# Perceiver, two layers on one core: normed rows, softmax sums, key spreading and sine transfers of layer 0 in another order

## The chip, the cores and the metric

The kernel runs on 1 core of one Trainium2 chip. The metric is the device time of one execution in microseconds (us). The core has five engines that run side by side, each with its own queue of instructions, worked off strictly in order: TensorE (PE in the profile), VectorE (DVE), ScalarE (ACT), GpSimd (POOL) and SyncE (SP, which here only starts transfers). They wait for each other through semaphores.

## The reference, cut to what matters

The model is a perceiver with two layers over x (64 sequences of 32 rows, 256 wide) and a context (64 x 257 rows). Layer 0, which is all that the change touches, is

```python
x = x + xattn(layernorm(x), ctx)      # 16 heads of 16, rotary q and k, a window of 64 keys back
x = x + attn(layernorm(x))            # 16 heads, rotary, causal
x = x + fp8_linear(layernorm(x))
```

With 32 rows in a sequence, both attentions reach only keys 0 to 31 and are causal. Layer 1 (attention over all 257 context rows, a gated mixer, a mixture of 8 experts and a shared one) follows in the same program.

## The kernel before, in words

The 2048 rows of x lie in SBUF as four groups of 512 rows (`xs[0..3]`), each four tiles of 128 rows. `small_attentions` (line 246) does both attentions of layer 0 as one list of eight steps, `order`: four groups of the first attention, then four of the second. A step has four turns, t = 0 to 3; a turn is one 128-row tile.

The program writes the order of every engine out by hand. The loop at line 542 is a software pipeline: a turn computes the scores of tile T, and does the later stages of the tiles before it, held in `line`. Per tile:

- `scores` (392): 8 masks and 32 small matmuls into one pair of PSUM banks ("b34", a single buffer, so the next tile's scores wait until this one's have been read), then on VectorE `mx` (row maximum) and `sc` (subtract it), then on ScalarE `e` (exponential).
- `sums` (434), one turn later: VectorE adds up `e` per head and takes the reciprocal, `sm`.
- `turned` and `context` (440, 452), two turns later: TensorE transposes `e` into `ps_t`, ScalarE copies it (`eT`), 32 matmuls with the values give `ps_o`, VectorE scales it by `sm` into `o`.
- `by_feature` (475), three turns later: `o` is transposed (`ps_c`), ScalarE copies it with a bias (`cT`).
- `project` (487), four turns later: `ps_p`, which VectorE adds to x. `ps_o`, `ps_c` and `ps_p` share two PSUM banks.

Beside this, a step prepares the next one, called `after`. `opened` (298) transposes its normed rows y (`psT`) and ScalarE copies them (`yT`), at t = 0. `rotated` (304) is called four times, (1,0), (1,1) for keys and (0,0), (0,1) for queries: a projection `ps_qk`, then VectorE multiplies it by the sine (`part`), four transfers of 64 KB each move `part` by 32 partitions into `far`, ScalarE copies `ps_qk` to `near`, GpSimd multiplies `near` by the cosine, and one turn later GpSimd adds `near` and `far` into `kT` or `qT`. `spread_keys` (343) writes four masked copies of a piece of `kT` into `kb`, three on ScalarE and one on GpSimd, in two parts per turn. `values` and `blocks` (360, 380) project the values, write them to DRAM (`v_rows`) and load them back in another shape (`vb`).

In the second attention keys come from `yT`; in the first they come from the context, so only its queries need `yT`.

The layer norm is `norm_steps` (123), spread over the four turns of the step two ahead: statistics at t = 0; aggregation and a Newton iteration for the reciprocal root at t = 1 (on GpSimd, except in the first groups, where VectorE does it); normed rows y of tiles 0 and 1 at t = 2, of tiles 2 and 3 at t = 3. With `by_act` ScalarE writes y as x * r + off, where GpSimd has made `off` = -mean * r with two small operations; without it, VectorE writes y = (x - mean) * r. Five of the eight steps (n = 1 to 5) have `by_act`; their rows are opened at the start of steps 2 to 6. Also on VectorE, a few `scratch` operations per step decode the fp8 weights in n = 1 to 4.

Before the loop comes a start (from line 492): loads, normed rows of group 0, its four `rotated` (where VectorE makes `near`, too), the first spreading, both `values`. In these four calls half of the sine transfers are started from ScalarE's queue. `eye`, a small selection matrix that the scores need, is made by VectorE from the constants `cst`, ahead of the first norm.

The turn's order at line 560 is `turned`, `sums`, the first part of `spread_keys`, at t = 0 the owed additions and `opened`, `project`, `rotated`, `by_feature`, the norm's piece, the additions, the second part of `spread_keys`, `values` or `blocks`, `scores`, `context`.

Of the kernel before, what the change touches and what calls it, by code (L numbers as in the profile page):

```python
# [12 lines left out]
ALU = mybir.AluOpType  # L13
# [5 lines left out]
NB, S, SK = 64, 32, 257  # L19
# [45 lines left out]
def perceiver_kernel(ctx: ExitStack, tc: tile.TileContext, a: dict, out: bass.AP):  # L65
# [15 lines left out]
    ident = cst[:, C_ID : C_ID + P]  # L81
# [16 lines left out]
    class InOrder:  # L98
# [12 lines left out]
    vector, scalar, gpsimd, sync = (  # L111
        InOrder(e) for e in (nc.vector, nc.scalar, nc.gpsimd, nc.sync)
    )
# [115 lines left out]
    def proj(ps, w, rhs):  # L229

        for k in range(2):
            mm(ps, lhsT=w(k), rhs=rhs(k), start=(k == 0), stop=(k == 1))
# [13 lines left out]
    def small_attentions(layers, first_loads, decode, sides, load_layer1, layer1):  # L246
# [24 lines left out]
        def mask(which):  # L271
            at = C_CAUSAL[which]
            mk = sb.tile([P, 8, S], BF16, tag=f"lx{which}", name=f"mk{which}")
            scalar.copy(mk, cst[:, at : at + S][:, None, :].to_broadcast([P, 8, S]))
            masks.append(mk)
# [17 lines left out]
        def group(n, kvT):  # L293

            layer, g = order[n]
            return dict(layer, n=n, g=g, kvT=kvT)

        def opened(it):
            yT = transposed(it["y"], pa, yTs([P, 2, GT], "yT"))
            it["yT"] = yT  # L300
            if not it["from_ctx"]:
                it["kvT"] = yT

        def rotated(it, i, c):

            src, cs, sn = (
                (it["kvT"], cos, sin) if i == 1 else (it["yT"], cosq, sinq)
            )
            place = "kT" if i == 1 else "qT"
            if c == 0:  # L310
                it[place] = kT_all if i == 1 else qT_([P, 2, GT], "qT")
            dst = it[place]
            w, v0 = it["w"], it["v0"]
            ps = pa([P, GT], "ps_qk")
            proj(ps, lambda k: w[:, i, k, c * P : (c + 1) * P], lambda k: src[:, k, :])

            def by_place(table):
                return table.rearrange("p (o q) -> p o q", o=1).to_broadcast([P, 16, S])

            def by_seq(tile_):  # L320
                return tile_.rearrange("p (b q) -> p b q", q=S)

            bias = vec[:, v0 + 2 * i + c : v0 + 2 * i + c + 1]
            part = part_([P, GT], "part")
            vector.scalar_tensor_tensor(
                by_seq(part), by_seq(ps), bias, by_place(sn), ALU.add, ALU.mult
            )

            far = far_([P, GT], "far")
            for at in range(0, P, S):  # L330
                queue = scalar if it["n"] == 0 and at >= 2 * S else sync
                queue.dma_start(out=far[at : at + S, :], in_=part[at ^ S : (at ^ S) + S, :])
            near = near_([P, GT], "near")
            if it["n"] > 0:
                scalar.activation(near, ps, AF.Identity, bias=bias)
                gpsimd.tensor_tensor(by_seq(near), by_seq(near), by_place(cs), ALU.mult)
            else:
                vector.scalar_tensor_tensor(
                    by_seq(near), by_seq(ps), bias, by_place(cs), ALU.add, ALU.mult
                )  # L340
            return lambda: gpsimd.tensor_tensor(dst[:, c, :], near, far, ALU.add)

        def spread_keys(it, half, c, part):

            if (c, part) == (0, 0):
                it["kb"][half] = sb.tile(
                    [P, 2, NBT // 2, 4, S], F32, tag=f"kb{half}", name="kb"
                )
            kb, kT = it["kb"][half], it["kT"]
            src = kT[:, c, half * D : (half + 1) * D].rearrange("p (b k) -> p b k", k=S)  # L350
            for h in range(2 * part, 2 * part + 2):
                mine = m4r[:, h : h + 1]
                if h != 1:
                    scalar.activation(kb[:, c, :, h, :], src, AF.Copy, scale=mine)
                else:
                    gpsimd.tensor_scalar(
                        kb[:, c, :, h, :], src, mine, 1.0, ALU.mult, ALU.mult
                    )
# [75 lines left out]
        def sums(tile_s):  # L434
            sm = small.tile([P, H], F32, tag="sm", name="sm", bufs=4)
            vector.tensor_reduce(sm, tile_s["e"], AX.X, ALU.add)
            vector.reciprocal(sm, sm)
            tile_s["sm"] = sm
# [55 lines left out]
        order = [(layer, g) for layer in layers for g in range(NG)]  # L494
# [5 lines left out]
        eye = sb.tile([P, S], BF16, tag="eye", name="eye")  # L500
        loads = first_loads()
        next(loads)
        it = group(0, fetch(0))
# [3 lines left out]
        for half in range(2):  # L507
            clear(vbs[1][half])
        scalar.copy(ident_bf, ident)
        vector.tensor_tensor(eye, ident[:, 0:S], ident[:, 64 : 64 + S], ALU.add)  # L510
        mask(0)
        it["y"] = finish(norm_steps(order[0][1], vector))
        it["kb"] = [None, None]
        adds = [rotated(it, 1, 0)]
        opened(it)
        mask(1)
        steps = norm_steps(order[1][1], vector, apart=True)
        next(steps)
        adds.append(rotated(it, 1, 1))
# [19 lines left out]
        line = [None] * 5  # L539
        adds = []  # L540
        layer1_loads = load_layer1()
        for n in range(len(order) + 1):
            if n >= last:
                after = None
            elif n > 0:
                after = group(n + 1, kvT)
                after["y"] = y
            if after is not None:
                after["kb"] = [None, None]
            kvT = None  # L550
            if n + 2 <= last:
                side = norm_steps(
                    order[n + 2][1], None if n else vector, apart=True, by_act=n > 0
                )
            else:
                side = sides
            y = None
            for t in range(NT):
                if line[2]:
                    turned(line[2])  # L560
                if line[1]:
                    sums(line[1])
                kb_now = None
                if n <= last:
                    if t < 2:
                        kb_now = (now, 1, t)
                    elif after is not None:
                        kb_now = (after, 0, t - 2)
                if kb_now:
                    spread_keys(*kb_now, 0)  # L570
                due, adds = adds, []
                if t == 0:
                    for add in due:
                        add()
                    due = []
                    if after is not None:
                        opened(after)
                if line[4]:
                    project(line[4])
                if after is None:  # L580
                    next(layer1, None)
                elif t > 0:
                    adds.append(rotated(after, *((1, 1), (0, 0), (0, 1))[t - 1]))
                if line[3]:
                    by_feature(line[3])
                if n + 2 <= last:
                    try:
                        next(side)
                    except StopIteration as end:
                        y = end.value  # L590
                else:
                    next(side, None)
                    next(side, None)
                if n > 0:
                    add_bias(n - 1, t)
                if n > 0 and t != 1:
                    next(decode, None)
                for add in due:
                    add()
                if kb_now:  # L600
                    spread_keys(*kb_now, 1)
                if after is None:
                    next(layer1, None)
                elif t == 0:
                    adds.append(rotated(after, 1, 0))
                elif t < 3:
                    values(after, t - 1)
                else:
                    for half in range(2):
                        blocks(after, half)  # L610
                line[0] = scores(now, t) if n <= last else None
                if (n, t) == (last, NT - 1):
                    pair_pool.close()
                    later_psum.append(
                        attention.enter_context(tc.tile_pool(name="at_late", bufs=1, space=PSUM))
                    )
                if line[2]:
                    context(line[2])
                if t == 0 and n + 2 <= last:
                    kvT = fetch(n + 2)  # L620
                elif n < 2:
                    next(loads, None)
                elif n >= last - 2:
                    next(layer1_loads, None)
                line = [None] + line[:-1]
            now = after
# [1415 lines left out]
```

## Time and profile before

| what | value |
|---|---|
| three runs | 946.12, 948.07, 949.11 us (median 948.07) |
| the profiled execution | 949.13 us, its span 947.4 us |
| busy in the span | PE 861.0, DVE 588.5, POOL 501.4, ACT 433.7 us |

| stretch, us | what | PE busy | DVE busy | ACT busy | POOL busy |
|---|---|---|---|---|---|
| 0 to 36 | start, up to the first scores | 20.82 | 18.86 | 9.20 | 13.63 |
| 36 to 62 | step 0 and a stall at its end | 18.43 | 17.60 | 14.09 | 11.81 |
| 62 to 110 | steps 1 and 2 | 45.22 | 33.10 | 28.70 | 30.22 |
| 110 to 215 | steps 3 to 6 | 94.03 | 79.33 | 69.46 | 71.45 |
| 215 to 260 | step 7 and the passage to layer 1 | 38.79 | 34.11 | 19.66 | 20.80 |
| 260 to 781 | rest of layer 0 and layer 1's attention | 494.83 | 364.95 | 261.37 | 284.29 |
| 781 to 947 | experts | 148.88 | 40.58 | 31.27 | 69.23 |

A row of a list of groups or of a timeline gives a start, a duration, the engine, the operation and the tiles that it writes and reads; in brackets stands how long the engine was idle before it and whose work ended that. SPq and ACTq are the engines' transfer-issuing instructions. Matmul ends are modelled, so a busy PE may hide small stalls.

### The profile page before, as it was taken

The page shows a single profiled execution, that of the slowest core. Times are in us where ns is not written, and L with a number is a line of the kernel's source. Part 1 is how long each engine was busy: PE and PEld are TensorE (multiplying, and loading weights), DVE is VectorE, ACT ScalarE, POOL GpSimd, SP SyncE. Part 2 cuts the span into 40 slices and gives each one's busy share as a digit, 9 for nine tenths or more (in the row PEclk, how much of TensorE's full clock was granted, in tenths as well). Part 3 has the DMA queues.
Part 4 walks back from the last instruction along what each step waited for, and adds up shares of the span by engine and source line. Part 5 has one row for each costly group of instructions (what it writes and reads, how often), then busy time and mean ns, then how long its engine had stood idle before and what let it go on. Part 6 is the DMA issues. An engine that isn't in the chain of part 4 may idle for free. (4 is left out here: it accounts for less than half of the span.)

```text
span 947.4 us, 22812 instructions
## 1 busy us (share of the span) xinstructions
PE 861.0 (91%) x8699; PEld 589.2 (62%) x8699; DVE 588.5 (62%) x1733; ACT 433.7 (46%) x1119; POOL 501.4 (53%) x994
## 2 busy tenths in 40 slices
PE   5779889987989999999999999999889889999993
PEld 2546566665546666566666656565566648888882
DVE  4757777788667748766776757678763781121116
ACT  1457666665365545554554546554444222222210
POOL 3447666675395647647565647655651204455430
PEclk9989999999999999999999999999799989999997
DMA  5564332344301111101111113000001035777658
GB/s 156 149 157 130 85 77 75 95 125 147 100 7 51 52 52 51 48 5 52 52 52 51 53 51 95 3 1 2 24 24 35 23 127 170 236 230 243 213 184 266
DMA packets 66718, 88.79 MB, mean 94 GB/s; under 512 B 32400, under 2 KB 49840, under 8 KB 64560
## 3 DMA queue, kind: packets, MB, share of 16 engines
q1 hardware_dynamic: 62768, 77.36, 27.1%
q0 software_dynamic: 3456, 9.44, 3.0%
q8 instruction: 69, 1.13, 0.5%
q10 hardware_dynamic: 384, 0.52, 0.2%
q14 instruction: 41, 0.34, 0.1%
HBM read 65.80 MB, written 13.11 MB: 83 GB/s over the span
## 5 line engine op out<-in xcount | busy, mean ns | idle before, releaser
L106 ACT ACTIVATE e<-e,xnm 128x257 f32<-128x257 f32 x256 | 127.2, 498 | 51.1 <-DVE xnm L106 47.7
L106 DVE CUSTOM_DVE_ANT_0 e<-ps_s,mask 128x257 f32<-128x257 f32 x256 | 93.4, 420 | 50.1 <-PE ps_s L118 49.8
L118 PE MATMUL ps_k<-ct,w_w_l1x 128*128 128x512 f32 x256 | 122.3, 600 | 1.5 <-ACT yT L106 0.5
L118 PE MATMUL ps_v<-w_w_l1x,ct 128*128 128x256 f32 x512 | 121.9, 381 | 0.0
L106 POOL TENSOR_SCALAR e<-e,xsm 128x256 f32<-128x256 f32 x256 | 121.2, 492 | 0.0
L121 PE MATMUL ps_t<-cst,e 128*128 128x128 f32 x640 | 103.2, 284 | 7.8 <-DVE eT L106 6.9
L106 DVE COPY eT<-ps_t 128x512 f32<-128x512 f32 x128 | 87.9, 687 | 28.5 <-PE ps_t L121 28.1
L118 PEld LDWEIGHTS ps_v<-w_w_l1x,ct 128*128 128x128 f32 x512 | 94.0, 192 | 11.0 <-issue 0.2
L106 POOL TENSOR_TENSOR x<-x,rows 128x256 f32<-128x256 f32 x96 | 70.4, 749 | 44.0 <-ACT y L106 16.9
L106 ACT ACTIVATE kT<-ps_k,vec 128x512 f32<-128x512 f32 x64 | 44.0, 688 | 100.8 <-PE ps_k L118 100.5
L121 PEld LDWEIGHTS ps_t<-cst,e 128*128 128x128 f32 x640 | 72.2, 142 | 26.3 <-DVE eT L106 7.6
L106 ACT ACTIVATE hTr<-ps_h,w 128x256 f32<-128x256 f32 (+1 forms) x80 | 31.3, 449 | 115.3 <-issue 88.1
L106 DVE TENSOR_TENSOR og<-ps_o,b 128x512 f32<-128x512 f32 (+1 forms) x20 | 12.8, 638 | 104.5 <-PE ps_o L118 104.5
L118 PEld LDWEIGHTS ps_k<-ct,w_w_l1x 128*128 128x128 f32 x256 | 44.5, 190 | 41.3 <-issue 35.3
L1807 POOL DMA_INDIRECT r_rows<-og,lv x36 | 35.5, 986 | 61.2 <-DVE og L106 56.3
L118 PE MATMUL ps_h<-ygT,w 128*128 128x256 f32 (+1 forms) x320 | 65.8, 359 | 0.6 <-issue 0.6
L118 PE MATMUL ps_o<-w,hTr 128*128 128x256 f32 x288 | 65.3, 379 | 0.0
L106 ACT COPY v<-ps_v 128x512 f32<-128x512 f32 x80 | 46.3, 580 | 39.4 <-PE ps_v L118 37.9
L106 POOL TENSOR_TENSOR near<-near,cst 128x512 f32<-128x512 f32 x28 | 35.9, 1282 | 53.2 <-ACT near L106 51.9
L106 POOL TENSOR_TENSOR last<-e,xsm 128x4 f32<-128x4 f32 x64 | 12.9, 202 | 89.2 <-DVE xsm L106 89.2
L106 ACT ACTIVATE kb<-kT,cst 128x256 f32<-128x256 f32 x96 | 45.3, 513 | 30.9 <-POOL kT L106 20.6
L118 PEld LDWEIGHTS ps_h<-ygT,w 128*128 128x128 f32 x320 | 54.9, 190 | 6.6 <-issue 0.8
(209 smaller groups left out, 1693.2 us busy)
## 6 DMA issues: line engine op xcount, KB each, us to landing
ct<-in_ctxT SPq DMA_DIRECT2D x16, 1024.0 KB
w<-in_ew SPq DMA_DIRECT2D x20, 514.0 KB
w<-in_ew SPq DMA_DIRECT2D x20, 512.0 KB
far<-part SPq DMA_DIRECT2D x120, 64.0 KB
v_rows<-v SPq DMA_DIRECT2D x16, 256.0 KB
vb<-v_rows SPq DMA_DIRECT2D x64, 64.0 KB
r<-r_rows SPq DMA_DIRECT2D x8, 512.0 KB
b<-in_eb SPq DMA_DIRECT2D x20, 128.0 KB
```

The costliest lines, as they stand in the source:

```text
L106: ins = getattr(self.engine, name)(*args, **kw)
L118: return kept(nc.tensor.matmul(ps, **args))
L121: return kept(nc.tensor.transpose(ps, src, eye))
L1807: wrote = nc.gpsimd.indirect_dma_start(out=r_rows, out_offset=bass.IndirectOffsetOnAxis(ap=write_i[:, at : at + 1], axis=0), in_=o[:, i, : ...
```

## The change

Five edits, all in `small_attentions`: all sine transfers of the start go to SP's queue; `eye` is made after the first normed rows, `rotated(1,0)` and `opened`; `by_act` is gone there, so VectorE writes y in every step (GpSimd still does the Newton iteration); in each turn, `sums` comes last, behind `context`, instead of near the top; and at t = 0 the first part of `spread_keys` comes behind the owed additions and `opened`. For t > 0 nothing stands between the old and the new place of `spread_keys`.

```diff
             for at in range(0, P, S):
-                queue = scalar if it["n"] == 0 and at >= 2 * S else sync
-                queue.dma_start(out=far[at : at + S, :], in_=part[at ^ S : (at ^ S) + S, :])
+                sync.dma_start(out=far[at : at + S, :], in_=part[at ^ S : (at ^ S) + S, :])
...
         scalar.copy(ident_bf, ident)
-        vector.tensor_tensor(eye, ident[:, 0:S], ident[:, 64 : 64 + S], ALU.add)
         mask(0)
         it["y"] = finish(norm_steps(order[0][1], vector))
         it["kb"] = [None, None]
         adds = [rotated(it, 1, 0)]
         opened(it)
         mask(1)
+        vector.tensor_tensor(eye, ident[:, 0:S], ident[:, 64 : 64 + S], ALU.add)
...
-                side = norm_steps(
-                    order[n + 2][1], None if n else vector, apart=True, by_act=n > 0
-                )
+                side = norm_steps(order[n + 2][1], None if n else vector, apart=True)
...
                 if line[2]:
                     turned(line[2])
-                if line[1]:
-                    sums(line[1])
...
-                if kb_now:
-                    spread_keys(*kb_now, 0)
                 due, adds = adds, []
                 if t == 0:
                     for add in due:
                         add()
                     due = []
                     if after is not None:
                         opened(after)
+                if kb_now:
+                    spread_keys(*kb_now, 0)
...
                 if line[2]:
                     context(line[2])
+                if line[1]:
+                    sums(line[1])
```

## The prediction

> **What bounds the kernel now.** I read the page first (shares, slices, the chain), then who waited for whom in steps 1 to 6, then timelines of the start and of one step's end. The chain that ended last runs on PE and VectorE only from 781 us and says nothing of layer 0, so layer 0 has to be read from waits. Waits there, 64 to 215 us (engine, what, what it waited for: us in total, times, longest):
>
> ```profile
> DVE sm L106 <- ACT e L106: 23.8, 23, 2.8
> ACT kb L106 <- POOL kT L106: 18.3, 6, 4.0
> PE ps_qk L118 <- ACT yT L106: 6.1, 4, 1.5
> PE psT L121 <- ACT y L106: 4.1, 10, 0.7
> PE ps_o L118 <- DVE x L106: 2.0, 5, 0.4
> PE ps_p L118 <- ACT cT L106: 1.2, 3, 0.7
> ```
>
> PE is the bound: in turns 1 and 2 its operations follow without a gap (scores at 171.33, 177.72 and 184.11 us: 6.39 us a turn). It stands only around the change of step, in turns 3 and 0: 13.4 us of listed waits in five such changes, on three things that the change touches: y written by ScalarE, `yT` behind other ScalarE work, x behind VectorE's wait for `e`. That wait of 23.8 us delays everything that VectorE has queued behind `sums`. One change of step (timeline; start, duration):
>
> ```profile
> 185.83 1.09 ACT L106 ACTIVATE y<-x,off,rn 128x256 f32<-128x256 f32 x2
> 188.75 0.69 DVE L106 TENSOR_REDUCE sm<-e 128x16 f32<-128x512 f32 x1 [2.14 <-ACT e L106]
> 190.15 0.65 PE L118 MATMUL ps_o<-vb,eT 128*32 128x64 f32 x32 [0.39 <-DVE x L106]
> 191.84 1.09 ACT L106 ACTIVATE y<-x,off,rn 128x256 f32<-128x256 f32 x2
> 192.50 0.33 PE L121 MATMUL psT<-cst,y 128*128 128x128 f32 x1 [0.67 <-ACT y L106]
> 194.60 0.52 ACT L106 ACTIVATE kb<-kT,cst 128x256 f32<-128x256 f32 x1
> 195.01 1.07 ACT L106 COPY yT<-psT 128x512 f32<-128x512 f32 x2
> 196.13 1.98 PE L118 MATMUL ps_qk<-yT,w_w_l0a 128*128 128x512 f32 x4 [1.52 <-ACT yT L106]
> ```
>
> ScalarE is the chain here: y, `kb`, `v`, `e`, `eT`, `kb`, `near`, `cT`, y, `kb`, `e`, `eT`, `kb`, `yT` back to back, but for the 1.15 us in which `near` waits for VectorE's `part`.
>
> The start (timeline):
>
> ```profile
> 9.80 0.19 DVE L106 TENSOR_TENSOR eye<-cst 128x32 bf16<-128x32 f32 x1 [9.80 <-DMA cst<-in_consts]
> 14.47 2.08 PE L121 MATMUL psT<-cst,y 128*128 128x128 f32 x8 [1.65 <-DVE y L106]
> 16.08 1.50 ACTq L106 DMA_DIRECT2D far<-part  x2
> 21.43 7.83 ACTq L106 DMA_DIRECT2D far<-part  x6
> 29.31 2.50 ACT L106 ACTIVATE kb<-kT,cst 128x256 f32<-128x256 f32 x6 [10.32 <-DMA far<-part]
> 32.34 0.66 PE L121 MATMUL psT<-cst,y 128*128 128x128 f32 x4 [2.70 <-ACT v L106]
> ```
>
> VectorE can't begin the norm until the constants land, though only `eye` needs them. ScalarE is stuck for 7.83 us issuing transfers whose `part` isn't ready, so spreading and value copies start at 29.31 and the first scores end at 35.49.
>
> **The start, part by part.** (1) Norm: from the first statistics (9.91) to the last y (15.39) takes 5.48 us; x was asked for at 0.74, two loads ahead of the context rows that PE received at 9.07. If x lands by about 7, y is ready by 12.5, before PE ends its first projection at 12.82, and nothing waits for it; the trace doesn't show x's landing, only that it is ahead of 9.07, and at 9.07 the start would lose 1.2 us of the gain. So `psT` follows at 12.82 instead of 14.47, and `part`(1,0) comes at about 12.9 instead of 15.30. (2) Sine transfers: SP alone issues four of a call in 2.4 us (row at 42.52: 2.44 for 4) where SP and ScalarE took 1.5 together, +0.9 on each call's landing. `kT`'s first addition came 1.7 us behind the last issue: 12.9 + 0.7 + 2.4 + 1.7 = 17.7 against 19.27. (3) The second key projection waits for PE alone: 14.9 + 1.9 to 3.75 us (below), so its `part` comes at 16.9 to 18.7 against 20.64. Then 0.7 for `near`, 3.7 for the second group's Newton iteration (21.97 to 25.68), and both query calls: `part`(0,0) at 22.0 to 23.8 against 25.68. SP is free by then and issues eight in 4.9 us: 27.6 to 29.4; plus 1.9 to land, plus 1.26 for the addition: `qT` complete at 30.8 to 32.6, against 32.08 before. That is the price of (2), and it makes `qT` the last to arrive: ScalarE's spreading (from 19 us), value copies (by 26) and PE's `psT` (26 instead of 32.34) are now earlier. First scores end 0.35 later: 31.2 to 32.9 instead of 35.49. `v_rows`, behind the eight issues on SP, start at 27.7 to 29.5 instead of 32.31. Gain 2.8 to 4.6 us; I take the middle, **3.7**.
>
> The two ends differ by PE's clock. After idling, PE ran at half speed: the four matmuls at 16.85 took 3.75 us, equal ones at 32.83 1.97; full speed came at 20.40, 5.9 us after `psT` began, and after the stall at 62.21 some 6 us later again. Now PE runs without a pause from 9.07, so full speed may come by 15. The Trainium skill ("TensorE: Matmul & The Clock Gate", Part 1 and Part 4) has a free-running window of about 3.4 us of sustained work, and says that transposes don't count as such; by it the eight transposes would leave the second projection slow, the low end, 2.8. No row here tells transposes from matmuls.
>
> In step 0 SP issues without a break (39.28 to 61.8, gaps under 0.5) and PE stands 6.06 us at 56 to 62 for a `far` that queued behind 772 KB of `rows`. Both begin with `v_rows`, so the stall moves with the start and stays as long.
>
> **The change of step.** Replay of the rows at 184 to 196, all durations from them:
> - GpSimd loses the two `off` operations (at 181.88 and 182.16, 0.44 us with gaps), so `kT` and ScalarE's `kb` (184.35) come at 183.9.
> - ScalarE loses 1.0 us at each y pair. 20 y's of 602 ns leave it; VectorE gains 20 of 410 ns (the median of its own y's), 1.6 us a step, beside a wait for `e` of 4 to 5 us a step that goes. GpSimd's r is ready at 181.92, VectorE reaches y at 182.9.
> - Turn 2 on VectorE: `part` ends 182.9, then two y. Alone 0.73; beside GpSimd's operations they are slower (row at 203.26: four took 2.40), so 0.7 to 2.0. `sc` ends at 186.7 to 188.1 instead of 186.28; the next scores want the bank at 188.6, so PE doesn't see it. `e` runs at 187.0 to 188.1 (188.08 before).
> - `sums` (0.95 us) stands behind `o` and waits for nothing; x, `part` of turn 3 come at 188.1 to 188.8 (189.64 before), held by `ps_qk`, which ends at 188.4. y pair 0.73 (GpSimd is idle 2.21 us there), `mx`, `sc` to 191.5 to 192.0, `near` at 189.5, `cT` to 191.2.
> - PE: `ps_p` 0.3 earlier, no wait at `ps_o`, `psT` from 190.3 without a gap, `ps_p` at 191.4 instead of 193.36. ScalarE: `near`, `cT`, `kb`, `e`, `eT`, `yT` (now ahead of `kb`, 0.46 us) end at 193.8 to 194.2 instead of 196.08.
>
> So `ps_qk` comes 1.9 to 2.3 us earlier. Next late are `qT` (GpSimd adds it by about 195.8, the new scores at 195.7) and ScalarE itself. The same replay at 84 to 88, where `ps_qk` doesn't need `yT`, gives 1.9. Price for the five changes: 1.9 each, **9.5**; bounds 1.0 (just the listed waits for y and x) to 2.3.
>
> Spreading behind the copies delays GpSimd's share of `kb` by one addition, 1.27 us; it is read two turns later. In turns without y, moving `sums` removes VectorE waits of 0.36 us in front of a wait for PE (0.31): nothing. Behind layer 0 all work is in order of data, DMA is at 0 to 3 tenths until the experts, and the shift carries to the end.
>
> **Sum.** 949.13 - 3.7 - 9.5 = 935.9 for the profiled execution; its time lies 1.06 above the median, so 934.9, say **935**. Bounds of the terms: gains 1.6 + 5.0 to 4.6 + 11.5, so 932 to 941.5 by the median.
>
> **Rivals.**
> - *Only the start gains* (14%): the second queue takes the place of the first; ScalarE's order or a late `far` holds `ps_qk` where it is. For it: `qT` did wait 0.62 us for `far` at 195.78. Against: `part`, which feeds `far`, gets earlier too. 948.1 - 3.7 = 944.4.
> - *The start gains nothing* (8%): eight issues on one queue, 4.9 us, cancel the earlier norm (x lands late, PE stays slow). 938.6.
> - *Slower* (9%): y on VectorE collides with GpSimd. VectorE's y took 383 ns at best, 1430 at worst. If every y pays 1.43, a pair costs 2.86: turn 2's `sc` ends at 188.9, just at the next scores; turn 3 then has x at 190.6 (`ps_o` 0.45 late), y to 194.1, `sc` 195.5, `yT` about 197.7 instead of 196.08: +1.6 per change, +8.0, less 3.7: 952.4. It decides from about 1.9 us a pair in both turns. Against: in turn 3 GpSimd waits for `near`. The Trainium skill ("SBUF — State Buffer", "Who interferes with whom") has such a rule: one-source VectorE operations in a two-port mode and GpSimd operations exclude each other for a whole instruction. The trace agrees in places (`w` at 183.23 took 1.37 and ended 0.28 behind GpSimd's `kT`).
> - *Nothing to measure* (3%): y's cost and the shorter waits cancel.
>
> **How the numbers follow.** Forecast, both terms: 66%. A measurement here can tell about 0.3%, 2.8 us, from no change. Faster by more: 66 + 8 + most of the first rival, 84%; within: 7%; slower: 9%. Range 928 to 945: the bounds, widened below for waits that I took as staying, above to hold the first rival.
>
> **What would show it.** Right: first scores end before 33; no `psT` wait for y and `ps_qk` wait for `yT` under 0.5 us; steps 3 to 6 shorter by 2 each; y on VectorE near 0.4 to 0.7. Wrong: a new PE wait for `qT` or `sc`, y's of over 1 us in turn 3, first scores at 35.

## The result and the profile after

The changed kernel takes 936.82 us (median of 4 runs, 935.21 to 937.20) against 948.59 us before (4 runs, 946.12 to 949.30): ratio 0.988, 95% interval 0.986 to 0.990. That is 11.8 us less. The profiled execution took 937.20 us, 11.9 less than the one shown of before.

Waits of after in the same five steps (58 to 208 us here; engine, what, what it waited for: us in total, times, longest):

```profile
ACT e L106 <- DVE sc L106: 15.7, 17, 1.7
...
PE ps_qk L118 <- ACT yT L106: 4.9, 4, 1.3
...
PE ps_c L121 <- DVE o L106: 3.1, 3, 1.1
```

The first of them stood in before, too (64 to 215 us):

```profile
ACT e L106 <- DVE sc L106: 10.1, 13, 1.7
```

VectorE's wait for `e` (23.8 us) and PE's waits for y and x are gone. ScalarE's wait for `sc` has grown from 10.1 to 15.7 us, and PE has a new one for `o`; both tiles are written by VectorE. The wait for `yT` has hardly shrunk, 4.9 instead of 6.1.

The same change of step as shown of before, now at 180 to 187 (timeline; start, duration):

```profile
180.86 0.73 DVE L106 TENSOR_SCALAR y<-x,mv,rn 128x256 f32<-128x256 f32 x2
...
182.22 0.69 DVE L106 TENSOR_TENSOR sc<-pair_bank,mx 128x512 f32<-128x512 f32 x1
...
182.94 0.63 ACT L106 ACTIVATE e<-sc 128x512 f32<-128x512 f32 x1
...
183.95 1.08 ACT L106 COPY yT<-psT 128x512 f32<-128x512 f32 x2
...
185.08 1.98 PE L118 MATMUL ps_qk<-yT,w_w_l0a 128*128 128x512 f32 x4 [0.89 <-ACT yT L106]
```

Here everything goes as it was meant to. Three steps earlier (timeline of after, 101 to 111):

```profile
101.73 0.73 DVE L106 TENSOR_SCALAR y<-x,mv,rn 128x256 f32<-128x256 f32 x2
...
102.68 1.27 POOL L106 TENSOR_TENSOR near<-near,cst 128x512 f32<-128x512 f32 x1 [1.28 <-ACT near L106]
102.82 1.41 DVE L106 TENSOR_TENSOR scratch<-scratch 128x256 f32<-128x256 f32 x1
...
104.87 0.69 DVE L106 TENSOR_TENSOR sc<-pair_bank,mx 128x512 f32<-128x512 f32 x1
...
105.94 0.44 PE L121 MATMUL ps_c<-cst,o 128*128 128x128 f32 x2 [1.11 <-DVE o L106]
106.60 1.08 ACT L106 COPY yT<-psT 128x512 f32<-128x512 f32 x2
...
107.73 3.43 PE L118 MATMUL ps_qk<-yT,w_w_l0a 128*128 128x512 f32 x4 [1.35 <-ACT yT L106]
```

A decoding operation (`scratch`) follows y in VectorE's queue. It begins 0.14 us behind GpSimd's multiplication of `near`, takes 1.41 us instead of some 0.4, and ends 0.28 behind it. So `sc` and `o` are late, PE stands twice (1.11 and 1.35 of 2.9 us), and then four matmuls take 3.43 us instead of 1.98, most of it at half speed (the mean granted clock from 107.7 to 111.2 is 0.57).

The length of a step shows the same, from the first mask of a step to that of the next (us, from the timelines; the last two columns are runs told below):

| step | before | after | e1: decoding moved | e9: y on ScalarE |
|---|---|---|---|---|
| 2 | 27.49 | 27.35 | 24.33 | 25.46 |
| 3 | 26.85 | 27.26 | 24.12 | 25.45 |
| 4 | 26.96 | 24.52 | 24.25 | 25.59 |
| 5 | 26.84 | 24.12 | 24.24 | 25.44 |

Steps 1 to 4 have decoding in turn 3. In step 4 its two operations together take 0.49 us and are over when `near` has hardly begun; step 5 has none there (its last ones come in turns 0 and 2). Only those two got shorter by more than 0.2 us. Behind steps 1 and 3 the second decoding operation is stretched as it is behind step 2, 1.41 us at 78.53 and, in the timeline of after,

```profile
130.17 1.28 DVE L106 CAST scratch<-scratch 128x256 int32<-128x256 f32 x1
```

The start of after (timeline):

```profile
4.71 1.41 DVE L106 BATCH_NORM_STATS2 st<-x 128x6 f32<-128x256 f32 x4 [4.71 <-DMA x<-in_x]
...
12.86 1.91 PE L121 MATMUL psT<-cst,y 128*128 128x128 f32 x8
...
22.29 4.97 SPq L106 DMA_DIRECT2D far<-part  x8
...
28.87 1.26 POOL L106 TENSOR_TENSOR qT<-near,far 128x512 f32<-128x512 f32 x1 [1.19 <-DMA far<-part]
...
30.19 0.45 PE L118 MATMUL pair_bank<-kb,qT 64*32 64x128 f32 x16 [1.90 <-POOL qT L106]
```

x lands by 4.71; `psT` follows the first projection without a gap; SP's eight transfers take 4.97 us, and `qT` is the last to arrive. The first scores end at 30.64 instead of 35.49.

From the timelines, the lead over before is 5.15 us when turn 1 of step 1 begins (65.96 against 71.11). The changes of step behind steps 1 to 5 add 1.0, 0.1, -0.4, 2.4 and 2.7, and what follows adds 0.9.

### The profile page after: what moved, and what is told of

It is laid out like the page before. It is cut to its first block, busy times and chain, and to the rows that moved or that the text cites. A ratio compares the mean times of both kernels' runs of the same rounds, so it can differ in the third digit from the quotient of the medians.

```text
span 935.4 us, 22797 instructions
## 1 busy us (share of the span) xinstructions
PE 858.9 (92%) x8699; PEld 590.2 (63%) x8699; DVE 598.3 (64%) x1753; ACT 425.6 (45%) x1099; POOL 503.1 (54%) x984
## 3 DMA queue, kind: packets, MB, share of 16 engines
q8 instruction: 69, 1.13, 0.5%
## 5 line engine op out<-in xcount | busy, mean ns | idle before, releaser
L106 DVE COPY eT<-ps_t 128x512 f32<-128x512 f32 x128 | 87.9, 687 | 27.8 <-PE ps_t L121 27.5
L1804 POOL DMA_INDIRECT r_rows<-og,lv x36 | 35.6, 989 | 61.0 <-DVE og L106 56.2
L118 PEld LDWEIGHTS ps_o<-w,hTr 128*128 128x128 f32 x288 | 54.4, 190 | 7.2
```

What stands on the lines that cost most here:

```text
L106: ins = getattr(self.engine, name)(*args, **kw)
L118: return kept(nc.tensor.matmul(ps, **args))
L1804: wrote = nc.gpsimd.indirect_dma_start(out=r_rows, out_offset=bass.IndirectOffsetOnAxis(ap=write_i[:, at : at + 1], axis=0), in_=o[:, i, : ...
```

## The experiments

All times are medians; a ratio is to the kernel before on the same chip, with its 95% interval. There the kernel before had 947.94 (beside e1 to e4), 948.22 (e5 to e8) and 949.39 us (e9 to e12), so a difference of 1 to 2 us between kernels of different groups says little.

| run | what | us | ratio, interval |
|---|---|---|---|
| e1 | after, decoding out of turn 3 | 927.89 | 0.979 (0.977 to 0.981) |
| e2 | before, the start's two edits | 942.49 | 0.994 (0.992 to 0.997) |
| e3 | before, the loop's three edits | 940.28 | 0.993 (0.990 to 0.995) |
| e4 | before, decoding out of turn 3 | 950.37 | 1.002 (1.001 to 1.004) |
| e5 | before, sine transfers on SP alone | 943.42 | 0.996 (0.995 to 0.997) |
| e6 | before, `eye` later alone | 942.76 | 0.994 (0.993 to 0.996) |
| e7 | before, y on VectorE alone | 944.65 | 0.997 (0.995 to 0.999) |
| e8 | before, `sums` last alone | 941.70 | 0.994 (0.992 to 0.996) |
| e9 | after, y on ScalarE | 936.61 | 0.986 (0.983 to 0.989) |
| e10 | e1, `rows` loaded in two pieces | 929.21 | 0.978 (0.976 to 0.981) |
| e11 | after, decoding ahead of y | 934.77 | 0.985 (0.981 to 0.988) |
| e12 | e9, decoding out of turn 3 | 934.82 | 0.985 (0.983 to 0.988) |

**e1 and e4: the decoding.** The edit, in after (e1) and in before (e4):

```diff
-                if n > 0 and t != 1:
+                if n > 0 and t != 3:
                     next(decode, None)
```

> The changed kernel, with the fp8 decoding's pieces in turns 0, 1 and 2 of a step instead of 0, 2 and 3. Theory A (a decoding operation behind y in turn 3 meets GpSimd's multiplication of `near`, takes 1.3 to 1.4 us instead of 0.3 to 0.4, and holds `mx`, `sc` and `o`): the three changes of step behind steps 1 to 3, which gained 1.0, 0.1 and -0.4 us, now gain about 2.5 each like the other two, so 936.8 - 6.8 = 930, with no PE wait for `o` left there and `ps_qk` at full clock. Theory B (these three are held by something else, such as GpSimd's own additions or the loads of those steps): the wait goes to the next thing and the time stays at 936 to 937.

> The kernel before with the decoding moved out of turn 3 as in the first run. Theory A: in the kernel before ScalarE was the chain at the change of step and VectorE had slack, so the decoding in turn 3 cost little; moving it gives 0 to 2 us, 946 to 948. Theory B', that decoding in turn 3 costs the same with or without the change: about 941.

e1 took 927.89 us with one line moved: 8.9 less than after, or 8.3 if each is taken against its own kernel before (20.1 and 11.8 less). (Its profiled execution took 933.84 us, 6 more than the median, so only places in layer 0 are read from it.) A change of step of e1 (timeline):

```profile
99.10 0.73 DVE L106 TENSOR_SCALAR y<-x,mv,rn 128x256 f32<-128x256 f32 x2
...
100.05 1.28 POOL L106 TENSOR_TENSOR near<-near,cst 128x512 f32<-128x512 f32 x1 [1.10 <-ACT near L106]
100.46 0.69 DVE L106 TENSOR_TENSOR sc<-pair_bank,mx 128x512 f32<-128x512 f32 x1
...
103.32 1.98 PE L118 MATMUL ps_qk<-yT,w_w_l0a 128*128 128x512 f32 x4 [0.89 <-ACT yT L106]
```

`sc` now starts 0.41 us behind `near` instead of 2.19, PE waits 0.89 once, `ps_qk` runs at full speed, and steps 2 to 5 take 24.1 to 24.3 us each. Theory A holds, theory B falls. The gain is larger than the 6.8 us expected: the steps from turn 1 of step 1 on account for 6.9 (timelines), and the rest stays open. e4 shows that the price belongs to the pair: in the kernel before, where y was ScalarE's, the move gained nothing. It cost about 2.4 us, which neither theory had; in turn 1 the decoding meets GpSimd too (two operations took 1.58 us at 95.48), and PE's waits for `cT` in that profile went from 1.2 to 3.1 us in five steps.

**e11: which operation is stretched?** The decoding's piece of turn 3 goes ahead of the norm's:

```diff
+                if n > 0 and t == 3:
+                    next(decode, None)
                 if n + 2 <= last:
                     try:
                         next(side)
...
-                if n > 0 and t != 1:
+                if n > 0 and t in (0, 2):
```

> The changed kernel with the decoding's piece of turn 3 ahead of the two y instead of behind them. Theory (what is last of the four operations meets GpSimd's multiplication of `near`): now the second y takes about 1.3 us, the decoding 0.3 to 0.4 an operation; `mx`, `sc` and `o` are as late as before, and PE also waits for y at `psT`: 936 to 939. Rival (the decoding operation is slow by its own kind): it takes 1.3 where nothing of GpSimd's runs, and y 0.4.

The timeline of e11, same place:

```profile
99.77 0.41 DVE L106 SCALAR_TENSOR_TENSOR scratch<-scratch 128x256 f32<-128x256 f32 x1
...
100.22 0.42 DVE L106 TENSOR_TENSOR scratch<-scratch 128x256 f32<-128x256 f32 x1
...
100.56 1.69 DVE L106 TENSOR_SCALAR y<-x,mv,rn 128x256 f32<-128x256 f32 x2
...
100.72 1.38 POOL L106 TENSOR_TENSOR near<-near,cst 128x512 f32<-128x512 f32 x1 [1.31 <-ACT near L106]
...
105.74 1.98 PE L118 MATMUL ps_qk<-yT,w_w_l0a 128*128 128x512 f32 x4 [1.34 <-ACT yT L106]
```

The same decoding operation takes 0.42 us now, and the two y take 1.69 instead of 0.73: whichever runs beside `near` pays. So the rival falls. The time, 934.77, lies below the 936 to 939 expected: steps 2 and 3 took 26.12 and 25.77 us instead of 27.35 and 27.26, because `ps_qk` stayed at full speed (1.98 us) behind the same wait of 1.34.

**e9 and e12: what is y on VectorE worth?** e9 is after without that edit (`by_act` back); e12 has e1's edit on top.

```diff
-                side = norm_steps(order[n + 2][1], None if n else vector, apart=True)
+                side = norm_steps(
+                    order[n + 2][1], None if n else vector, apart=True, by_act=n > 0
+                )
```

> The changed kernel with y written by ScalarE again (`by_act` back); start, `sums` and spreading stay changed. Theory: with the decoding left in turn 3, y on VectorE costs about 1.4 us at three changes of step against `sums` alone (27.3 against 25.9 us a step) and gains 1.6 at the two others, so this edit is worth about nothing inside the change: 936 to 938, steps of 26 us all along. By the prediction's step (y's 1.0 us on ScalarE was most of the 1.9 a change): 941 or more.

> The changed kernel with y on ScalarE again and the decoding out of turn 3. Theory: with y on ScalarE the decoding in turn 3 was hidden, so moving it gives nothing against the ninth run: 936 to 938; against the first run (927.9) this is then what y on VectorE is worth once nothing is queued behind it, about 8 to 9 us. Rival (the decoding costs the same wherever y is written): 930 or less.

e9 took 936.61 us, after 936.82: as it stands in the change, the edit is worth nothing that can be told. Its steps are 25.5 us all along: against them after gains 1.1 to 1.3 in steps 4 and 5 and loses 1.8 to 1.9 in steps 2 and 3. With the decoding out of the way it is worth 6.9 us (e12 934.82, e1 927.89), or 5.5 if each is taken against its own kernel before; 8 to 9 were expected. That the decoding alone is free with y on ScalarE can't be told finely (e9 and e12 overlap, and e12's steps are 0.1 to 0.2 us longer than e9's), but the rival's 930 is out.

**e2, e3, e7, e8: the parts.** e2 holds the start's edits of the diff above and nothing else, e3 the loop's; e7 and e8 one loop edit each, as in the diff.

> The kernel before with the two edits of the start alone (sine transfers on SP, `eye` later). By the traces the start is worth what the lead was behind the stall, 5.15 us: 948.1 - 5.2 = 943. By the prediction's step it is worth 3.7: 944.4. If part of the lead comes from the loop's edits in step 0, less: 946.

> The kernel before with the three edits of the loop alone (y on VectorE, `sums` last, spreading behind `opened`). By the traces the loop's edits are worth 12.0 - 5.15 = 6.9 us: 941.2. By the prediction's step 9.5: 938.6. If the two parts need each other, so that neither alone gives its share: 943 or more.

> The kernel before with only y written by VectorE, `sums` and the spreading in their old places. Theory: y in turn 3 no longer follows ScalarE's `kb`, and ScalarE is 1 us earlier with `yT`; but `part` and y stand behind VectorE's wait for `e`. Most of the loop's gain of 7.7 us: -4 to -5, 943.5. Rival (`sums` is what frees VectorE): 0 to -2, 947.

> The kernel before with only `sums` moved to the end of the turn. Theory: PE's waits for x (0.4 us in each of five changes of step) go, and `part` comes earlier, but y and `yT` stay ScalarE's: -1 to -2, 946.5. Rival: VectorE's wait for `e` holds everything behind it, so moving it gives the larger share, -4 or more, 944.

The start gave 5.5 us, the loop 7.7; their sum is a little more than the 11.8 of both. In the loop the expectation was upside down in the totals: `sums` alone gave 6.5, y alone 3.6. By their steps 2 to 5, which scatter less than whole runs do, `sums` alone takes 25.8 to 26.1 us, 1.0 less than before (1.4 in step 2), whatever the decoding does; y alone takes 26.9, 28.0, 25.9 and 24.6. So in step 5, where no decoding stands behind y, y alone gains 2.2 and `sums` alone 1.0: there the expectation was the right way up. That it is the decoding that turns the totals over fits steps 2 and 3, but wasn't tested by itself. From e8 to e9 (the start's edits and the spreading) a step gets 0.4 to 0.6 shorter; as e2's steps are those of before (27.5, 26.9, 27.0, 26.9), this is put down to the spreading behind `opened`, which wasn't run alone; one `kb` that stood ahead of `yT` takes as much (0.52 at 194.60 of before).

**e5 and e6: the start's two edits, each alone.**

> The kernel before with only the sine transfers of the start put on SP's queue. Theory: VectorE still starts its norm at 9.9 us, so `part` of the first query call still comes at 25.7; SP then issues eight in 4.9 us, `qT` is complete at 33.8 instead of 32.1, and the first scores end at 34.3 instead of 35.5: about -1.2 us, 946.8. Rival (ScalarE's 7.8 us in its queue were most of the start's loss): first scores by 32 and 943 to 944.

> The kernel before with only `eye` moved behind the first norm. Theory: the whole start moves with the norm. `part` of the first query call comes at 21.5 us, ScalarE is out of its transfers at about 24 instead of 29.3, the first scores end at about 30.7: -4.5 us, 943.5, nearly all that the two edits gave together (5.5). Rival (both are needed, since ScalarE's queue holds the spreading): -2 or less, 946.

The first scores end at 33.9 (e5) and 33.0 us (e6), both later than with both edits (30.6). Yet the times are 4.8 and 5.5 us lower than before, nearly the 5.5 of both. The stall in step 1 tells why. Before, after, then e6 (timelines):

```profile
62.21 0.68 PE L118 MATMUL pair_bank<-kb,qT 64*32 64x128 f32 x16 [6.06 <-POOL qT L106]
```

```profile
55.96 1.26 POOL L106 TENSOR_TENSOR qT<-near,far 128x512 f32<-128x512 f32 x1 [6.76 <-DMA vb<-v_rows]
...
57.28 0.68 PE L118 MATMUL pair_bank<-kb,qT 64*32 64x128 f32 x16 [7.26 <-POOL qT L106]
```

```profile
56.13 1.26 POOL L106 TENSOR_TENSOR qT<-near,far 128x512 f32<-128x512 f32 x1 [2.40 <-DMA far<-part]
...
57.45 0.45 PE L118 MATMUL pair_bank<-kb,qT 64*32 64x128 f32 x16 [2.59 <-POOL qT L106]
```

(The first row of after names a `vb` transfer; the addition reads only `near` and `far`, and the last `far` stands just ahead of `vb` in the same queue.) The stall ends at 57.3 to 57.7 us in after, e5 and e6 alike (62.2 before); who comes to it earlier waits longer. So expectation and rival of both runs asked about the wrong place: as far as these traces show, the start's worth is how much earlier the queue of transfers is through, not when the first scores end.

The end of the stall also scatters from kernel to kernel with the same start. With one or both of the start's edits (and all of `rows` loaded in step 0) it lies between 55.9 (e12) and 57.7 us (e5) in eight profiles; with neither, between 59.7 (e8) and 62.2 (before) in five. The profile of before is the latest of its five, so the lead of 5.15 us, read from one pair of profiles, is uncertain by some 2 us; the medians of e2, e5 and e6 are firmer.

**e10: a shorter queue.** Of `rows` only the first 256 columns, which steps 1 to 4 need, are loaded in step 0, the rest in turn 1 of step 2; otherwise it is e1.

```diff
-        sync.dma_start(out=rows, in_=a["rows"].partition_broadcast(P))
+        sync.dma_start(
+            out=rows[:, 0:R_AO0], in_=a["rows"].partition_broadcast(P)[:, 0:R_AO0]
+        )
...
+        yield
+        yield
+        sync.dma_start(
+            out=rows[:, R_AO0:N_ROW], in_=a["rows"].partition_broadcast(P)[:, R_AO0:N_ROW]
+        )
...
-                elif n < 2:
+                elif n < 3:
                     next(loads, None)
```

> The first run's kernel (decoding out of turn 3), and of `rows` only the first 256 columns loaded in step 0 (128 KB), the other 644 KB in step 2. Theory: PE's stall of 5 to 7 us in step 1 is the backlog of big loads ahead of the last `far` of step 0; with 644 KB less it ends about 3 to 4 us earlier: 924. Rival (the backlog is x's third load and the many small `vb` reads, or the loads moved to step 2 give it back there): 927 to 928.

The stall ended at 54.5 us (56.2 in e1), and turn 1 of step 1 began 1.5 us earlier; of the median nothing is left (ratio 0.978 and 0.979). With 644 KB less the wait is 3.9 us instead of 5.6; the end lies only 1.4 us outside the scatter told above, and most of the wait is still there, so these bytes are not the whole backlog. What else it is, and where the 1.5 went, stays open. e1 is the fastest kernel here, and e10 can't be told from it.

## Why the prediction was right, and where not

It said 935, and 936.82 came. The direction and the two terms hold (e2 and e3 show both gains), but each term was off, in opposite directions: the start gave 1.5 to 1.8 us more and the changes of step 3.7 less. That the sum came within 2 us is in part luck.

- **Start, 3.7 predicted; 5.15 by the traces, 5.5 in e2.** Right: x lands early, `psT` at 12.86, eight issues in 4.97 us, `qT` the last to arrive, full clock by about 15, so the warm end. First scores ended before 33, at 30.64, under the 31.2 to 32.9 given. Wrong: "the stall moves with the start and stays as long". It got 1.2 us longer and seems to end where the transfers are through (e5, e6). The term was too small by some 30%; it came that near because a shift of the start also shifts the queue.
- **Changes of step, 9.5 predicted; 5.8 by the traces.** "1.9 each" fits none: the two clean ones gave 2.4 and 2.7, the three others 1.0, 0.1 and -0.4.
- **The step that failed** is "y pair 0.73 (GpSimd is idle 2.21 us there), `mx`, `sc` to 191.5 to 192.0". The 0.73 is right; what stands behind y in VectorE's queue was left out. The replay was made at a change without decoding in turn 3 (behind step 5) and multiplied by five; the second one, at 84 to 88, has two decoding operations in its rows (84.22 and 84.54, 0.28 and 0.29 us), but gave the same 1.9 where 1.0 came. In steps 1 to 3 a decoding operation fills the rest of GpSimd's idle time and runs into `near`. e1 gives the price: 8.3 to 8.9 us, more than the shortfall, since clean changes bring more than 1.9.
- **The clean ones gained more** because three edits each had a share there: `sums` 1.0 (e8), spreading about 0.4, y 1.1 to 1.3 (after against e9). The prediction took ScalarE's y for the chain and gave `sums` only the 0.4 at `ps_o` and an earlier `part`. These shares depend on the order: alone, y gave 2.2 in step 5 (e7), so that taking it for the chain was right for a clean change.
- **The rival "slower: y collides with GpSimd"** had the right mechanism at the wrong operation. It was ruled out "in turn 3" because GpSimd waits there; that cover lasted 1.28 us, and `part` and y used it up. The Trainium skill ("SBUF — State Buffer", "Who interferes with whom") has, beside the rule that the prediction used, one for VectorE operations with two SBUF inputs: they contend with GpSimd instructions that read SBUF. The traces agree with both: the stretched operation behind step 2 has two inputs (TENSOR_TENSOR, 1.41 beside `near`), those behind steps 1 and 3 are casts with one (1.41 and 1.28), as y in e11 has one, while `sc` (0.69, at 104.87) and `o`, which read PSUM, kept their time beside GpSimd's `qT`. The `w` that the prediction gives for the rule of one source has two inputs, so it bears on the other rule.
- **Signs.** The `psT` wait for y went, as said. y took 0.73 a pair in turn 3 and 1.50 to 1.52 in turn 2, within the 0.7 to 2.0 given. Of "steps 3 to 6 shorter by 2 each" steps 4 and 5 came (2.4 and 2.7); step 3 got 0.4 longer. `ps_qk`'s wait for `yT` did not fall under 0.5: it is 0.89 at best (step 5, and e1), because `sc`, `e`, `eT`, `yT` still follow one another. A new PE wait "for `qT` or `sc`" was named as a sign of error; one came, at `ps_c` for `o`, which stands right behind `sc` on VectorE.

## What to carry to other kernels

When a piece of work changes its engine, replay every turn that it lands in, not one of them, with what is queued behind it there: small work that was free in the old order may now stand in the way, and moving it can be worth more than the edit. Count the time until the other engine's next operation, not only that it is idle now. And where a stall behind a queue of transfers follows, an earlier arrival at it is worth only what the queue itself moves.

## What the runs showed of the hardware

- **Two short waits can halve PE's clock.** In the 14 profiles, a wait of 1.13 to 1.53 us directly ahead of `ps_qk` at a change of step, with none over 0.7 us near it, was followed by full speed in all 38 cases of twelve kernels. A wait of 0.97 to 1.15 for `o` and one of 1.34 to 1.74 for `yT`, with 0.44 us of work between, were followed by half speed in 5 of 6 (after, e3, e7): 3.4 to 3.8 us instead of 1.98; the sixth, in e7 (1.15 and 1.74), ran at full speed. A wait of 1.76 in the passage to layer 1, the same in every kernel, was followed by half speed in 3 of 14; in e1 (timeline):

```profile
240.25 0.54 PE L121 MATMUL ps_c<-cst,o 128*128 128x128 f32 x2 [1.76 <-DVE xnm L106]
...
240.58 3.52 PE L118 MATMUL ps_k<-ct,w_w_l1x 128*128 128x512 f32 x4
```

  So waits that add up to 1.8 to 2.7 us in some 3 us can cost about 1.5 more, but not each time: behind the single wait of 2.59 us in e6, shown above, PE ran at full speed. The Trainium skill ("TensorE: Matmul & The Clock Gate", "Why this matters for your kernels") asks for gaps under about 3 us; here shorter ones were enough. Its free-running window (Part 1) would fit the chance; no run here shows where that window lies.
- **Transposes did not keep PE slow.** In after PE began at 9.32; the eight transposes at 12.86 took 1.91 us, and the four matmuls right behind them 2.17, near full speed, where the low end of the start's term has 3.75. In e2 the transposes at 12.91 themselves ran at full speed, 1.04 us. This speaks against the low end.
